# Fused attention and mixture-of-experts block: the exponential tiles' sums without VectorE, with two tiles of a unit added by accumulating DMAs

## Chip, cores and metric

One core of a Trainium2 chip. Time is device microseconds of one execution of the whole program, the median of several runs. Of the engines, PE is the tensor engine, DVE is VectorE, ACT is ScalarE, POOL is GpSimd, and SP is SyncE, which only issues DMAs here.

## What is computed

A transformer block in float32 on x of shape (2, 1024, 512): attention with 16 heads of 32 and low-rank updates on its four projections, a residual and a layer norm; then a mixture of 8 experts (hidden size 704, at most 256 tokens for each) with a shared expert, a residual and a layer norm. The change concerns the softmax of the attention alone:

```python
q = _split(lora_linear(x, Wq, bq, Bq, Aq))
k = _split(lora_linear(x, Wk, bk, Bk, Ak))
v = _split(lora_linear(x, Wv, bv, Bv, Av))
scores = jnp.einsum('bhqd,bhkd->bhqk', q, k) * SCALE
attn = jax.nn.softmax(scores, axis=-1)
out = jnp.einsum('bhqk,bhkd->bhqd', attn, v)
...
x = _layernorm(x + _L0_attn_ref(x, ...), axis=-1)
x = _layernorm(x + _L0_ffn_ref(x, ...), axis=-1)
```

## The kernel before

The program has three stages: the projections of Q, K and V; the attention; and the experts with their routing. The attention is cut into 16 units. A unit `u` is four heads (group `g = u // 2`) and half of a batch's queries (512). Its 1024 keys are cut into 8 chunks of 128, and one chunk is a step; `t` counts the steps of all units, 128 in all, with `u = t // 8` and `k = t % 8`.

In a step, for each of the four heads, the tensor engine multiplies keys by queries into a bank `st` (line 604), ScalarE takes the exponential into an SBUF tile `pt` (line 613), and the next head follows. Two heads share a tile of 128 x 1024, so each step makes two tiles, called pair 0 and pair 1; below, "tile j" means the two tiles of step j of a unit. Softmax needs the maximum of each query's row beforehand. It comes from a second product, `s`, 12 steps ahead (`LEAD`; `s1_step`, lines 176 to 197): one matmul of 512 columns per head and step slot into one of three banks, reduced to its maximum by VectorE (line 191). The maxima reach the exponentials as two extra rows of Q, written by `finish_max`.

One step later, `av_step` (line 628) multiplies the tiles by V into the unit's `av` bank; there are two such banks, so that of unit u is also that of unit u - 2. The tiles are also summed over the steps, element by element (`add_step`, line 617): tile 0 is the accumulator itself, tiles 1 to 6 are added to it, 7 is left out (`DIRECT`). `ON_DVE` puts the adds of (step 1, pair 0) and (step 2, pair 1) on VectorE; the other ten of a unit are GpSimd's. The last two units have their own list, `DVE_END`. The adds are issued just behind `av_step`, except that `EARLY`, (1, 0), is issued one step sooner.

At step 3 (`FIN`) of the next unit `finish` (line 651) sums accumulator and tile 7 over the partitions by matmuls with ones into a bank `sm` (line 657). ScalarE copies `sm`, and SyncE sends one row of each head to DRAM and back as 128 x 16. After step 4 (`REC`) VectorE takes the reciprocal (`invert`, line 678), SyncE writes it to DRAM and reads it back broadcast over the partitions (four DMAs). At step 7 `normalize` (line 691) multiplies the `av` bank by it on VectorE, copies it on ScalarE, and subtracts on VectorE (the result is kept as a high and a low part). From unit `RDIR` on the reciprocal is taken of the whole bank by VectorE (line 667) and DRAM is not used.

The tensor engine's order is written by hand: `between[h]` holds what follows head h's `st` matmul in a step. All engines execute in program order. The `pt` tiles come from a pool of `PTB` = 13 buffers of 4 KB per partition. A buffer is free again when its last reader is done, which for most tiles is GpSimd's add. GpSimd's queue also holds one bias add of 128 x 512 in most units (`add_res`, line 707), and, in units 8 to 10, small operations of the first layer norm. Those units also carry the first batch's output projection (`oproj`, from `t` = 65), which reads the normalised units 0 to 7.

Of the kernel before, what the change touches and what calls it, by code (L numbers as in the profile page):

```python
# [2 lines left out]

# [6 lines left out]
F32 = mybir.dt.float32  # L10
# [3 lines left out]
ALU = mybir.AluOpType  # L14
# [4 lines left out]
P = 128  # L19
B, L, D = 2, 1024, 512  # L20
NU = 16
# [11 lines left out]
LEAD = 12  # L33
LATE, OP_ONE = (0,), 1
NS = NU * 8
WARM, WCOL = 4, 256
OPER = 4
PTB = 13
OHB = 3
LOADS = {  # L40
# [11 lines left out]
MAN4 = MAN2 - MAN3  # L52
DIRECT = (7,)
NO_DIR = (NU - 2,)
FIN = 3
REC = 4
XTB = 5
ON_DVE = ((1, 0), (2, 1))
EARLY = (1, 0)
OPROJ_AT = (65, 67, 69, 71, 73, 75, 77, 79)  # L60
RES_AT = tuple(8 * i + 6 for i in range(8)) + (70, 78, 86, 94, 98, 102, 106, 110)
RES_ADD = 3
# [3 lines left out]
W2_END = {2: (0, 1, 2), 3: (3, 4), 4: (5,)}  # L66
W2_AT = {2: (0, 1), 3: (2, 3), 4: (4,), 5: (5,)}
MPJ, MPP = 0, 2
RDIR = NU - 2
FINE, NRME = 2, 4  # L70
DVE_END = {
    NU - 2: ((1, 0), (2, 1), (4, 1), (5, 1), (6, 0), (6, 1), (7, 0), (7, 1)),
    NU - 1: ((1, 0), (2, 0), (3, 0), (4, 0), (5, 0), (6, 0), (6, 1)),
# [20 lines left out]
def kernel(  # L94
# [3 lines left out]
    pe, act, dve, pool, sp = nc.tensor, nc.scalar, nc.vector, nc.gpsimd, nc.sync  # L98

    def f(ap):  # L100
        return ap.bitcast(F32)
# [41 lines left out]
    def load_k(g):  # L143
        kt = Ks[g % 2]
        for blk, hl in ((0, 0), (1, 1), (2, 0)):
            sp.dma_start(
                out=f(kt[32 * blk : 32 * blk + 32]),
                in_=qk_d[1, g // NG, g % NG, hl].rearrange("(h p) t -> p h t", p=32),
            )
# [13 lines left out]
    def load_q(u):  # L163
        g, qb = u // 2, u % 2
        for blk, hl in ((0, 0), (1, 0), (2, 1)):
            sp.dma_start(
                out=f(Qs[u % 3][32 * blk : 32 * blk + 32]),
                in_=qk_d[0, g // NG, g % NG, hl].rearrange("(h p) t -> p h t", p=32)[
                    :, :, qb * 512 : qb * 512 + 512
                ],  # L170
            )

    mts, pts, avs, accs, vts = {}, {}, {}, {}, {}
# [411 lines left out]
    with ph2, tc.manual_schedule(engines={mybir.EngineType.PE}):  # L585
        ptp = att_left.enter_context(
            tc.tile_pool(name="ptp", bufs=PTB, side="left", reuse_waits="tile")
        )
        ap = ph2.enter_context(
            tc.tile_pool(name="ap", bufs=1, side="right", reuse_waits="tile")  # L590
        )
# [25 lines left out]
        def add_step(t, pr):  # L617
            u, kc = t // 8, t % 8
            if kc == 0:
                accs[u, pr] = pts[t, pr]  # L620
            elif kc not in direct(u):
                eng = dve if (kc, pr) in DVE_END.get(u, ON_DVE) else pool
                eng.tensor_tensor(accs[u, pr], accs[u, pr], pts[t, pr], ALU.add)  # L623

        def early(t, pr):
            return t // 8 not in DVE_END and (t % 8, pr) == EARLY

        def av_step(t):
            u, kc = t // 8, t % 8
            g = u // 2  # L630
            if kc == 0:
                avs[u] = avp.tile([P, 512], F32, name=f"av{u}", tag="av")
            for h in range(4):
                pe.matmul(  # L634
                    avs[u][32 * h : 32 * h + 32, :],
                    vts[g][:, kc, 32 * h : 32 * h + 32],
                    pts[t, h // 2][:, h % 2, :],
                    start=kc == 0,
                    stop=kc == 7,
                    skip_group_check=True,  # L640
                )
            for pr in range(2):
                if not early(t, pr):
                    add_step(t, pr)

        def direct(u):
            return () if u in NO_DIR else DIRECT
# [3 lines left out]
        def finish(u):  # L651
            sm = one.tile([P, 512], F32, name=f"sm{u}", tag="one")
            parts = [lambda h, k_=k_: pts[u * 8 + k_, h // 2][:, h % 2, :] for k_ in direct(u)]
            parts.append(lambda h: accs[u, h // 2][:, h % 2, :])
            for i, pf in enumerate(parts):
                for h in range(4):
                    pe.matmul(
                        sm[32 * h : 32 * h + 32, :],
                        ones32,
                        pf(h),  # L660
                        start=i == 0,
                        stop=i == len(parts) - 1,
                        skip_group_check=True,
                    )
            if u >= RDIR:
                rc = ap.tile([P, 512], F32, name=f"rc{u}", tag="rc", bufs=1)
                dve.reciprocal(rc, sm)
                fin[u] = rc
                return
            rc = ap.tile([P, 512], F32, name=f"rc{u}", tag="rc", bufs=1)  # L670
            act.copy(rc, sm)
            sd = dram.tile([4, 512], F32, name=f"sd{u}")
            sp.dma_start(out=sd, in_=rc[0:P:32, :])
            r16 = ap.tile([P, 16], F32, name=f"r16_{u}", tag="r16", bufs=1)
            sp.dma_start(out=r16, in_=sd.rearrange("h (j c) -> (h j) c", c=16))
            fin[u] = r16

        def invert(u):
            r16 = fin[u]
            rd = dram.tile([4, 512], F32, name=f"rd{u}")  # L680
            dve.reciprocal(r16, r16)
            sp.dma_start(out=rd.rearrange("h (j c) -> (h j) c", c=16), in_=r16)
            rc = ap.tile([P, 512], F32, name=f"rb{u}", tag="rb", bufs=1)
            for h in range(4):
                sp.dma_start(
                    out=rc[32 * h : 32 * h + 32, :],
                    in_=rd[h : h + 1, :].partition_broadcast(32),
                )
            fin[u] = rc

        def normalize(u, parts=(0, 1, 2)):
            g, qb = u // 2, u % 2
            cs = slice(qb * 512, qb * 512 + 512)
            hi, lo = at_h[:, g % NG, cs], at_l[:, g % NG, cs]
            if 0 in parts:
                dve.tensor_tensor(avs[u], avs[u], fin[u], ALU.mult)
            if 1 in parts:
                act.copy(hi, avs[u])
            if 2 in parts:
                dve.tensor_tensor(lo, avs[u], f(hi), ALU.subtract)  # L700

        def load_res(n):
            b, i = divmod(n, 8)
            r0 = b * L + i * P
            sp.dma_start(out=x1[b][:, i, 0:D], in_=x[r0 : r0 + P, :])
# [40 lines left out]
        for t in range(NS):  # L746
            u, k = t // 8, t % 8
            if k == 0:
                if u % 2 == 0 and 2 <= u and u // 2 + 1 < B * NG:
                    load_k(u // 2 + 1)  # L750
                if u >= 1 and u + 2 < NU:
                    load_q(u + 2)
                if u % 2 and NG <= u // 2 + 1 < B * NG:
                    load_v(u // 2 + 1)
            if t in RES_AT:
                load_res(RES_AT.index(t))
            between = [[], [], [], []]
            if early(t, 0):
                between[2].append(lambda: add_step(t, 0))
            if t + LEAD < NS:  # L760
                for q in range(4):
                    between[q].append(lambda q=q: s1_step(t + LEAD, q))
            elif t + LEAD == NS:
                between[0].append(lambda: finish_max(NU - 1))
            if t:
                between[1].append(lambda: av_step(t - 1))
                if u and k == (FINE if u == NU - 1 else FIN):
                    between[1].append(lambda: finish(u - 1))
            if u:
                if k == (NRME if u == NU - 1 else 7):  # L770
                    between[0].append(lambda: normalize(u - 1, (0,)))
                    between[1].append(lambda: normalize(u - 1, (1,)))
                    between[2].append(lambda: normalize(u - 1, (2,)))
            if t - RES_ADD in RES_AT:
                between[3].append(lambda: add_res(RES_AT.index(t - RES_ADD)))
            st_step(t, between)
            if k == REC and 1 <= u < NU - 1:
                invert(u - 1)
            if t in OPROJ_AT:
                op0 = oproj(0, OPROJ_AT.index(t), OPER)  # L780
            if OPROJ_AT[0] <= t:
                next(op0, None)
            if t + 1 in OPROJ_AT[1:]:
                run(op0)
            for _, fn in [x for x in later if x[0] == 0]:
                fn()
            later[:] = [(n - 1, fn) for n, fn in later if n]
            if t - NS >= OPROJ1:
                next(op10, None)
        av_step(NS - 1)  # L790
        finish(NU - 1)
        normalize(NU - 1, (0,))
        run(op10)
# [301 lines left out]
    for st in range(NB):  # L1095
# [18 lines left out]
        if st == NB - 3:  # L1114
            reads_xd(
                sp.dma_start(
                    out=meta, in_=xd_d[:, D : D + 2].rearrange("(j p) c -> p j c", p=P)
# [7 lines left out]
    with tc.manual_schedule(engines=MAN4):  # L1125
        last = None
        for e in range(E):
            nxt = e + 1
            hss = []
            for c in range(6):  # L1130
# [40 lines left out]
                if e:  # L1171
                    for hf in range(2):
                        j = 2 * (e - 1) + hf
# [9 lines left out]
        for hf in range(2):  # L1183
            j = 2 * (E - 1) + hf
# [65 lines left out]
```

## Time and profile before

| | us |
|---|---|
| median of 3 runs | 1081.89 |
| lowest and highest | 1078.75, 1085.99 |
| the profiled execution, and its span | 1070.33, 1068.6 |
| attention, from the first `st` to the last `av` matmul | 157 to 627 |

| engine | busy us of the span | share |
|---|---|---|
| tensor engine (matmuls) | 1038.4 | 97% |
| VectorE | 747.8 | 70% |
| GpSimd | 574.7 | 54% |
| ScalarE | 530.4 | 50% |

These shares are over three stages with different limits. The slices of the page divide the span by 40, so that one digit is 26.7 us, about one unit of attention; a digit is the busy share in tenths. A row of a group gives line, engine, operation, output and inputs with their shapes, the count, then busy time and mean duration in ns, then the engine's idle time just before these instructions and what ended it. The granted clock of the tensor engine is 0.991 of full speed in the mean. Matmuls are pipelined: an `st` or `s` matmul shows 0.40 us, but the next one starts 0.235 us after it.

### The profile page before, as it was taken

The page shows a single profiled execution, that of the slowest core. Times are in us where ns is not written, and L with a number is a line of the kernel's source. Part 1 is how long each engine was busy: PE and PEld are TensorE (multiplying, and loading weights), DVE is VectorE, ACT ScalarE, POOL GpSimd, SP SyncE. Part 2 cuts the span into 40 slices and gives each one's busy share as a digit, 9 for nine tenths or more (in the row PEclk, how much of TensorE's full clock was granted, in tenths as well). Part 3 has the DMA queues.
Part 4 walks back from the last instruction along what each step waited for, and adds up shares of the span by engine and source line. Part 5 has one row for each costly group of instructions (what it writes and reads, how often), then busy time and mean ns, then how long its engine had stood idle before and what let it go on. Part 6 is the DMA issues. An engine that isn't in the chain of part 4 may idle for free. (4 is left out here: it accounts for less than half of the span.)

```text
span 1068.6 us, 16466 instructions
## 1 busy us (share of the span) xinstructions
PE 1038.4 (97%) x5994; PEld 744.8 (70%) x5994; DVE 747.8 (70%) x1217; ACT 530.4 (50%) x1026; POOL 574.7 (54%) x379
## 2 busy tenths in 40 slices
PE   8999999999999999999999999999999999999996
PEld 6888774444444455554444358889999999999995
DVE  6732787899999987889999785333532457777762
ACT  5422214666666655556666656222322356665552
POOL 5000007888888887768998577000050026776674
PEclk9999998999999999999999999999999999999999
DMA  9866860141414242043520113000073356677731
GB/s 301 278 220 202 256 190 21 42 105 47 110 51 110 71 111 71 15 97 71 120 81 22 52 40 127 23 10 21 21 236 120 108 168 228 241 251 258 251 104 60
DMA packets 77585, 131.24 MB, mean 123 GB/s; under 512 B 14344, under 2 KB 23048, under 8 KB 77504
## 3 DMA queue, kind: packets, MB, share of 16 engines
q1 hardware_dynamic: 73664, 117.59, 37.1%
q0 software_dynamic: 3840, 12.60, 3.2%
q8 instruction: 47, 0.77, 0.3%
q14 instruction: 34, 0.28, 0.1%
HBM read 96.10 MB, written 33.80 MB: 122 GB/s over the span
## 5 line engine op out<-in xcount | busy, mean ns | idle before, releaser
L623 POOL TENSOR_TENSOR pt<-pt,pt 128x1024 f32<-128x1024 f32 x151 | 360.4, 2413 | 206.3 <-ACT pt L613 189.1
L191 DVE TENSOR_REDUCE mt<-s 128x1 f32<-128x512 f32 x512 | 323.8, 681 | 42.5 <-PE s L183 42.4
L613 ACT ACTIVATE pt<-st 128x512 f32<-128x512 f32 x512 | 270.9, 602 | 144.1 <-PE st L604 140.3
L604 PE MATMUL st<-qs,ks 98*128 98x512 f32 x512 | 216.4, 433 | 1.9 <-ACT pt L613 1.2
L183 PE MATMUL s<-ks,qs 96*128 96x512 f32 x512 | 204.1, 406 | 12.8 <-DVE mt L191 11.9
L604 PEld LDWEIGHTS st<-qs,ks 98*128 98x128 f32 x512 | 96.5, 190 | 137.3 <-issue 89.1
L864 PE MATMUL h<-xthe,w13s 128*128 128x256 f32 x704 | 129.9, 284 | 0.0
L183 PEld LDWEIGHTS s<-ks,qs 96*128 96x128 f32 x512 | 97.9, 191 | 41.4 <-DVE mt L191 26.9
L852 POOL TENSOR_TENSOR w2s<-w2r,w2s 128x512 fp32r<-128x512 f32 x42 | 65.9, 1592 | 96.9 <-ACT w2s L851 96.7
L864 PEld LDWEIGHTS h<-xthe,w13s 128*128 128x128 f32 x704 | 110.7, 191 | 0.3
L864 PE MATMUL h<-xtle,w13s 128*128 128x256 f32 x352 | 100.2, 285 | 0.0
L623 DVE TENSOR_TENSOR pt<-pt,pt 128x1024 f32<-128x1024 f32 x43 | 91.4, 2132 | 3.4 <-ACT pt L613 2.9
L634 PE MATMUL av<-pt,vt 128*32 128x512 f32 x512 | 75.0, 605 | 0.0
L634 PE MATMUL av<-pt,x1b 128*32 128x512 f32 x512 | 69.9, 619 | 0.0
L1012 POOL DMA_INDIRECT xd_d<-x1a,slot_i x8 | 8.0, 996 | 112.0 <-DVE slot_i L1009 109.9
L864 PEld LDWEIGHTS h<-xtle,w13s 128*128 128x128 f32 x352 | 67.4, 191 | 0.7
L908 PE MATMUL y<-w2s,hs 128*128 128x512 f32 x260 | 60.9, 390 | 0.0
L908 PEld LDWEIGHTS y<-w2s,hs 128*128 128x128 f32 x260 | 48.2, 188 | 10.2 <-DVE hs L890 0.5
L310 PE MATMUL o<-xl,wh 128*128 128x512 f32 x128 | 50.8, 397 | 0.9 <-POOL xl L296 0.9
L310 PE MATMUL o<-xh,wh 128*128 128x512 f32 x128 | 50.7, 396 | 0.8 <-ACT xh L295 0.8
L325 ACT ACTIVATE oh<-o,bqk_sb 128x512 fp32r<-128x512 f32 x32 | 22.0, 690 | 59.1 <-PE o L310 55.9
L310 PE MATMUL o<-xh,wl 128*128 128x512 f32 x128 | 50.5, 394 | 0.0
(822 smaller groups left out, 1760.2 us busy)
## 6 DMA issues: line engine op xcount, KB each, us to landing
qs<-qkd SPq DMA_DIRECT2D x48, 256.0 KB, 5.7
ks<-qkd SPq DMA_DIRECT2D x24, 512.0 KB, 6.9
x1a<-in_w_dram SPq DMA_DIRECT2D x24, 512.0 KB, 6.1
w2r<-in_w_dram SPq DMA_DIRECT2D x42, 256.0 KB, 2.9
qkd<-oh SPq DMA_DIRECT2D x32, 256.0 KB, 2.5
qkd<-ol SPq DMA_DIRECT2D x32, 256.0 KB, 2.5
x1b<-in_w_dram SPq DMA_DIRECT2D x16, 512.0 KB, 4.9
x1b<-in_wT_dram SPq DMA_DIRECT2D x16, 256.0 KB, 5.2
```

The lines of the kernel that those rows point to most:

```text
L183: pe.matmul(s1, Qs[u % 3][0:96, h, qt * P : qt * P + P], Ks[g % 2][0:96, h, kh * 512 : kh * 512 + 512], start=True, stop=True,)
L191: dve.tensor_reduce(mts[u][:, c, kh : kh + 1], s1, AX.X, ALU.max)
L310: pe.matmul(o, lhs, rhs, start=k + i == 0, stop=k + i == KC + 1)
L325: act.activation(oh, o, AF.Identity, bias=bias)
L604: pe.matmul(sb, Ks[g % 2][:, h, kc * P : kc * P + P], Qs[u % 3][:, h, :], start=True, stop=True,)
L613: act.activation(pts[t, h // 2][:, h % 2, :], sb, AF.Exp, scale=SCALE)
L623: eng.tensor_tensor(accs[u, pr], accs[u, pr], pts[t, pr], ALU.add)
L634: pe.matmul(avs[u][32 * h : 32 * h + 32, :], vts[g][:, kc, 32 * h : 32 * h + 32], pts[t, h // 2][:, h % 2, :], start=kc == 0, stop=kc == 7 ...
L852: pool.tensor_tensor(hl[:, 1, :], raw, f(hl[:, 0, :]), ALU.subtract)
L864: pe.matmul(hp[:, j * 256 : j * 256 + 256], lhs, rhs[:, k, :], start=n == 0, stop=n == 11,)
L908: pe.matmul(o, lhs, rhs, start=n == 0, stop=n == 16)
L1012: sc_ = pool.indirect_dma_start(out=xd_d, out_offset=bass.IndirectOffsetOnAxis(ap=slot_i[:, i : i + 1], axis=0), in_=x1[i // 8][:, i % 8, ...
```

## The change

The adds of each unit but the last two follow a table: `ADDS[kc]` lists the tiles whose adds are issued behind `av_step` of step kc. Tile 2 (both pairs) is not added to the accumulator: an accumulating DMA, issued from GpSimd, adds it into tile 3 after step 3's `av` matmuls have read that tile, and tile 3, which then holds both, is added by GpSimd after tile 4. So GpSimd has ten adds and two DMA issues in a unit, VectorE none. In unit 13 three tiles go by DMA (2 into 3, 4 into 5, 6 into 7), with six adds left for GpSimd. `finish` moves from step 3 to step 4, `invert` from after step 4 to after step 5, `normalize` from step 7 to step 0 of the unit after; unit 13 takes its reciprocal directly. `PTB` becomes 14, and the broadcast reciprocal uses the buffer that the copy of `sm` used.

```diff
-PTB = 13
+PTB = 14
-FIN = 3
-REC = 4
+FIN, FINQ = 4, 1
+REC = 5
+NRM = 0
-ON_DVE = ((1, 0), (2, 1))
-EARLY = (1, 0)
+ON_DVE = ()
+ON_DMA = {NU - 3: (2, 4, 6)}
+ADDS = {0: (0,), 1: (1,), 3: (2,), 4: (4,), 5: (3,), 6: (5,), 7: (6,)}
+ADDS_END = {0: (0,), 1: (1,), 3: (2,), 5: (4, 3), 7: (6, 5)}
...
-RDIR = NU - 2
-FINE, NRME = 2, 4
+RDIR = NU - 3
+FINE, NRME = 2, {NU - 2: 7, NU - 1: 4}
...
-            for pr in range(2):
-                if not early(t, pr):
+        def adds(t):
+            u, kc = t // 8, t % 8
+            if u in DVE_END:
+                for pr in range(2):
                     add_step(t, pr)
+                return
+            for j, pr in product((ADDS_END if u in ON_DMA else ADDS).get(kc, ()), range(2)):
+                i = u * 8 + j
+                if j in ON_DMA.get(u, (2,)):
+                    pool.dma_start(out=pts[i + 1, pr], in_=pts[i, pr], accum_op=ALU.add)
+                else:
+                    add_step(i, pr)
...
-            rc = ap.tile([P, 512], F32, name=f"rb{u}", tag="rb", bufs=1)
+            rc = ap.tile([P, 512], F32, name=f"rb{u}", tag="rc", bufs=1)
...
-            if early(t, 0):
-                between[2].append(lambda: add_step(t, 0))
...
                 between[1].append(lambda: av_step(t - 1))
+                between[3 if NS - 16 < t < NS - LEAD else 1].append(lambda: adds(t - 1))
                 if u and k == (FINE if u == NU - 1 else FIN):
-                    between[1].append(lambda: finish(u - 1))
+                    between[1 if u == NU - 1 else FINQ].append(lambda: finish(u - 1))
             if u:
-                if k == (NRME if u == NU - 1 else 7):
-                    between[0].append(lambda: normalize(u - 1, (0,)))
-                    between[1].append(lambda: normalize(u - 1, (1,)))
-                    between[2].append(lambda: normalize(u - 1, (2,)))
+                for v in [u - 2] * (k == NRM and 1 < u < NU - 1) + [u - 1] * (k == NRME.get(u)):
+                    between[0].append(lambda v=v: normalize(v, (0,)))
+                    between[1].append(lambda v=v: normalize(v, (1,)))
+                    between[2].append(lambda v=v: normalize(v, (2,)))
...
-            if k == REC and 1 <= u < NU - 1:
+            if k == REC and 1 <= u <= RDIR:
                 invert(u - 1)
...
         av_step(NS - 1)
+        adds(NS - 1)
         finish(NU - 1)
```

More of the change, by code (lines that the diff above doesn't have):

```diff
@@ L1 @@
 from contextlib import ExitStack
-from itertools import cycle
+from itertools import cycle, product
 import concourse.bass as bass
@@ L623, in add_step @@
                 eng.tensor_tensor(accs[u, pr], accs[u, pr], pts[t, pr], ALU.add)
-        def early(t, pr):
-            return t // 8 not in DVE_END and (t % 8, pr) == EARLY
         def av_step(t):
```

## The prediction

> **What bounds the kernel now.** I read the slices of the page first, then the costliest groups, then the timeline of one attention unit on the engines, and last the windows around the one place where the clock digit drops.
>
> ```profile
> PE   8999999999999999999999999999999999999996
> ...
> DVE  6732787899999987889999785333532457777762
> ...
> PEclk9999998999999999999999999999999999999999
> ```
>
> Attention runs from 157 to 627 us (slices 6 to 23): the tensor engine is at 9 throughout, but so is VectorE, at 9 or 8. A busy 9 on the tensor engine hides short stalls, so its steps have to be timed. I took the start of every fourth `st` matmul (L604), which is the start of a step. In units 1 to 7 the eight steps of a unit last, within 0.1: 3.08, 3.06, 3.48, 4.80, 3.96, 3.33, 3.06, 3.07; 27.84 us in all. An undisturbed step is 3.06. Step 3 also holds the 16 `sm` matmuls (about 1.73) and step 4 one transpose (0.24). So the tensor engine's own work is 8 x 3.06 + 1.73 + 0.24 = **26.45 us** and 1.39 us of each unit is stall, in steps 2, 4 and 5. The timelines of VectorE and of the tensor engine (start, us, engine, line, operation) show where it comes from:
>
> ```profile
> 283.50 1.28 DVE L191 TENSOR_REDUCE mt<-s 128x1 f32<-128x512 f32 x2
> 284.70 3.36 DVE L623 TENSOR_TENSOR pt<-pt,pt 128x1024 f32<-128x1024 f32 x1
> 287.98 1.27 DVE L191 TENSOR_REDUCE mt<-s 128x1 f32<-128x512 f32 x2
> ```
> ```profile
> 287.83 0.39 PE L604 MATMUL st<-qs,ks 98*128 98x512 f32 x1
> 288.71 0.50 PE L183 MATMUL s<-ks,qs 96*128 96x512 f32 x1 [0.49 <-DVE mt L191]
> ```
>
> While VectorE adds an exponential tile for 3.36 us, no maximum is taken; the three `s` banks fill, and the next `s` matmul starts 0.88 us after its `st` instead of 0.235. VectorE's reduces need only 2.48 us of a step, so without adds it keeps up. GpSimd is the other nearly full engine:
>
> ```profile
> L623 POOL TENSOR_TENSOR pt<-pt,pt 128x1024 f32<-128x1024 f32 x151 | 360.4, 2413 | 206.3 <-ACT pt L613 189.1 <-DVE pt L623 15.9
> ...
> L623 DVE TENSOR_TENSOR pt<-pt,pt 128x1024 f32<-128x1024 f32 x43 | 91.4, 2132 | 3.4 <-ACT pt L613 2.9 <-PE av L634 0.2
> ```
> ```profile
> 245.10:272.90 27.80, 27.19 (x146) 13.06 (x145) 25.76 (x40) 17.77 (x36) 24.70 (x12) 1.00 0.19 49
> ```
>
> In unit 3's window (columns: length, then PE, weight loads, VectorE, ScalarE, GpSimd, clock) GpSimd is busy 24.70 of 27.80, VectorE 25.76. The clock digit hides one event in unit 0:
>
> ```profile
> 170.51 0.40 PE L604 MATMUL st<-qs,ks 98*128 98x512 f32 x1
> 173.09 0.79 PE L183 MATMUL s<-ks,qs 96*128 96x512 f32 x1 [2.18 <-DVE mt L191]
> 173.81 1.94 PE L634 MATMUL av<-pt,x1b 128*32 128x512 f32 x8
> ```
> ```profile
> 178.00:180.00 2.00, 2.00 (x8) 0.93 (x11) 1.67 (x3) 1.37 (x3) 1.68 (x1) 0.50 0.06 18
> ```
>
> A VectorE add of 3.32 us at 169.12 starves the tensor engine for 2.18 us, and its clock is then 0.50 from about 173 to 183: steps 4 and 5 of unit 0 take 7.73 and 5.47 instead of 3.30 and 3.06.
>
> **What the skill says.** The Trainium skill, "SBUF — State Buffer", section on the two separate sides: a VectorE operation with two SBUF inputs and a GpSimd operation that reads SBUF take one port pair as an exclusive lock, and the second waits. The trace agrees: VectorE's add lasts 1.21 us at least, 1.90 in the median and 3.37 at most. "DMA: Bandwidth & Descriptors", section on SWDGE and HWDGE: an accumulating DMA can be issued from GpSimd only, whose cores write the descriptors. The trace has no accumulating DMA; it has GpSimd's indirect ones (below). The same page, anatomy of one DMA, prices a transfer at about 2.0 us + bytes / 436 GB/s. "TensorE: Matmul & The Clock Gate", part on the clock gate: idleness halves the clock until activity returns; the 0.50 after the 2.18 us gap agrees.
>
> **The change part by part.** (1) *VectorE's adds.* Two adds in each of units 0 to 13 go, 28 of 43; the 15 of units 14 and 15 stay. Worth the stalls, not the busy time. Above 26.45 units 1 to 7 have 9.8 us (27.83 + 27.91 + 27.84 + 27.83 + 27.86 + 27.81 + 27.86 - 7 x 26.45). Units 8 to 10 carry 96 output-projection matmuls at 0.235: 107.6 - (3 x 26.45 + 22.6) = 5.7. Units 11, 12 and 13 (27.81, 27.82, 28.28): 4.6. Sum **20.1**. (2) *Unit 0.* Steps 2, 4 and 5 are 0.5, 4.4 and 2.4 above: **7.3**, all behind a VectorE add; 2.2 of it is the stall itself and 4.7 the half clock, which I expect to go with it.
>
> (3) *GpSimd.* It keeps 10 adds in a unit (units 0 to 12): 10 x 2.34 (16.44 / 7 in a chain) = 23.4, one bias add of 1.2, and gains two DMA issues. Nearest row:
>
> ```profile
> L1012 POOL DMA_INDIRECT xd_d<-x1a,slot_i x8: 960/962/1232, 778.3 to 787.4; - x8
> ...
> DMA to landing us min/median/max: 3.4/6.6/8.1
> ```
>
> These are 128 rows as well, start to start 1.27 us. The accumulate reads two sources, so I take 1.2, with 0.6 and 2.0 as bounds. GpSimd then needs 23.4 + 1.2 + 2.4 = **27.0 us** of a unit of 26.45. It falls behind 0.55 in each unit. That is affordable: the issue follows the `av` matmuls of tile 3, done 14.2 us after the unit's start (four steps and 2.0); 2.4 and eight adds later, at 35.3, the unit's last add ends. The next unit's step 4 begins at 26.45 + 12.24 = 38.7, where an exponential first wants its buffer (by my count of the 14, one more than before), and the sums, moved from step 3 to 4, read it at about 40: some 4 us of slack. Units 1 to 7 use 3.9 of it; units 8 and 9 (38 and 40 us) give it back. Cost 0; with an issue of 2.0 us GpSimd needs 28.6, and 7 x 2.15 - 4 = 11 us are lost.
>
> (4) *The landing.* Tile 3 already waits for tile 2's DMA when GpSimd reaches its add, and everything behind it in GpSimd's queue waits too, then the sums, then the tensor engine. Between the first issue and that add lie the second issue and two adds of tile 4: 1.2 + 1.2 + 4.7 = 7.1 us. The scatters of L1012 move half as much and land in 3.4 alone and 6 to 8 when sixteen follow each other. Estimate from the page's price, twice the bytes read: 1.2 + 2.0 + 1.05 MB / 436 GB/s = 5.6. Lower bound 4, upper 11. Taken: in time, cost 0. The queue carries little at that point, since K and Q are loaded at step 0 (landing 5.7 to 6.9 us).
>
> (5) *Normalisation* from step 7 to step 0 of the unit after, one step before its `av` bank is written again. Before, its subtract ended 4.1 us after the start of its step; the same in step 0 reaches 1.05 into step 1, where `av` wants the bank at 1.06. Cost 0.1 to 0.5 a unit; I take 0.2. (6) *Reciprocal* one step after the sums, as before, but the steps between lose their stall: from the sums' end to it 5.9 us become about 5.2, the two small DMAs land at about 4.5, now beside 1 MB of accumulation. VectorE would wait in order with the reduces behind it. Cost 0 to 0.8; I take 0.3. (5) and (6): 12 x 0.5 = **6**.
>
> (7) *Units 13 to 15.* Unit 13 has three DMA pairs and six adds (14.0 + 7.2 us, less than now); its reciprocal becomes one of 3.36 us on VectorE in unit 14, where SyncE loses seven small DMAs and ScalarE a copy of 0.59. VectorE has gaps of 1.4 and 0.8 us near there. Cost 0, bounds -1 and 3; the stall in step 3 of unit 14 (5.95 us) stays, as VectorE's adds there do. After attention nothing changes, and the tensor engine is full there until 1000 us, so what attention gains arrives at the end.
>
> **Sum**: 20.1 + 7.3 - 6 = 21 us off the profiled execution's 1070.3 (span 1068.6): 1049. The median of the runs, 1081.9, is 11.6 above that execution for a reason that this profile cannot show; a clock event like that of unit 0 varies. I take a little less than the whole, 19, off the median: **1063**.
>
> **Rivals.** *(A) GpSimd's issue is dear or its landing late by 1 to 2 us*: a need of 28 to 29 a unit, the slack is used up by unit 3, 7 to 14 of the 21 us are lost: 1068 to 1075. For it: GpSimd is at 24.7 of 27.8 already. Against: the adds' own waits on VectorE (15.9 us in all) go. *(B) Slower: the landing of the accumulation.* Every unit's queue on GpSimd stops at tile 3's add. With a need of N per unit the loss is 7(N - 26.45) - 4 in units 1 to 7 and 2(N - 26.45) - 4 in units 11 and 12 against 21 gained, so it turns at N = 29.7: a stall of 2.7, a landing of about 10 us. At 13 us N is 33, the loss 51, the time about 1112. For it: 8.1 us for a quarter of a megabyte in a crowd; against: 2.8 to 3.4 for the same alone. *(C) The waits moved, not removed*: (5) and (6) at their upper ends, 1.3 x 12 = 16, and the clock event stays (4.7): 27 - 21 = 6 gained, 1076. *(D) The change doesn't do what it says*: the new order would leave the adds on VectorE or the tensor engine without slack; against it, the diff takes all 28 off VectorE, and 0.64 us of stall stands right behind one. Gain under 3, 1080.
>
> **Numbers.** Forecast with chance 0.60: 1054 to 1071. A 0.14, C 0.10, D 0.03, B 0.13. About 1% (10.8 us) is what a measurement of this kernel can tell from no change. Faster by more: the forecast and over half of A, 0.68. Within: the rest of A, C, D and the mild end of B, 0.19. Slower: 0.13. The range reaches from 1052 (no cost in 5 and 6, all of unit 0) to 1084, where B begins.
>
> **What would show it.** Right: units of about 26.5 to 27 us, steps 2 and 5 at 3.1, the 4.8 us step now number 4, no `s` matmul waiting on VectorE, VectorE near 21 of 26.7 us, the clock at 1.00 in unit 0, GpSimd above 95% busy. Wrong: gaps before tile 3's add released by the DMA, `sm` or ScalarE's exponentials waiting on GpSimd, `av` at step 1 waiting on the subtract, or a landing above 9 us.

## The result, and the profile after

| | before | after |
|---|---|---|
| median of 18 runs, us | 1079.67 | 1084.98 |
| lowest and highest | 1076.26, 1086.16 | 1080.61, 1089.43 |
| the profiled execution, its span | 1070.33, 1068.6 | 1084.36, 1082.7 |
| last `av` matmul of attention, us from the start | 627.8 | 627.4 |

The ratio is 1.0043 (95% interval 1.0027 to 1.006): the kernel is 0.4% slower, where 1.7% faster was forecast. The page of the kernel after, the slices that answer to those of before:

```profile
PE   9999999999999999999998999999989999999995
...
DVE  6742788778776877777677984323512467777752
...
PEclk9999999999999999999999999999979999999998
```

VectorE falls from 9 and 8 to 8 and 7 during attention, as meant, and the tensor engine's digits don't show that anything was gained. The costliest groups say that the work moved as planned (line, engine, operation, shapes, count | busy us, mean ns | idle before, releaser):

```profile
L626 POOL TENSOR_TENSOR pt<-pt,pt 128x1024 f32<-128x1024 f32 x147 | 366.0, 2904 | 159.3 <-PE av L634 142.6 <-ACT pt L616 12.2 <-DVE pt L626 3.7
...
L654 POOL DMA_DIRECT2D pt<-pt x32 | 29.4, 1092 | 36.7 <-PE av L634 24.4 <-PE st L607 5.1 <-DVE mt L194 4.9
L626 DVE TENSOR_TENSOR pt<-pt,pt 128x1024 f32<-128x1024 f32 x15 | 29.4, 1972 | 0.5
```

Fifteen adds are left on VectorE. GpSimd waits 24.4 us, in ten waits, before its DMA issue, for the `av` matmuls of tile 3: it has time to spare and is not the bound. The windows of a unit's length that begins 1.7 us into unit 3, of a place in unit 14, and of the place in unit 0 where the clock was 0.50 before (length, then busy time and count of the tensor engine, weight loads, VectorE, ScalarE, GpSimd; clock, DMA share, GB/s):

```profile
242.20:269.30 27.10, 27.10 (x149) 12.90 (x145) 21.64 (x38) 17.88 (x35) 26.36 (x14) 1.00 0.46 102
577.00:581.00 4.00, 4.00 (x15) 1.90 (x15) 2.62 (x6) 1.90 (x4) 2.25 (x2) 0.57 0.43 84
178.00:180.00 2.00, 2.00 (x13) 0.76 (x12) 1.70 (x3) 1.04 (x3) 2.00 (x3) 1.00 1.10 217
```

Unit 0's clock event is gone, and VectorE needs 21.64 us of a unit's length. But slow clock stands in a new place. As before I take the start of every fourth `st` matmul as the start of a step, and sum by unit:

| us | before | after |
|---|---|---|
| unit 0 | 32.7 | 25.6 |
| units 1 to 13 | 386.4 | 385.4 |
| units 14 and 15, to the last `st` | 49.6 | 56.1 |

Unit 0 gained its 7.1; units 1 to 13 gained 1.0 of about 14 to 20; units 14 and 15 lost 6.5. The units are now uneven. Outside units 8 to 10, odd ones take 26.9 to 27.5 (unit 1: 28.8), units 2 and 4 take 28.0, unit 6 takes 30.4, unit 12 takes 31.0. Step 4 is about 5.09 in odd units and 6.14, 6.17, 8.50 and 8.73 in units 2, 4, 6 and 12. The tensor engine's timeline in two of these steps, and in step 1 of unit 14 (start, us, engine, line, operation, then idle time before it and what ended it):

```profile
224.82 0.39 PE L607 MATMUL st<-qs,ks 98*128 98x512 f32 x1
226.03 0.47 PE L186 MATMUL s<-ks,qs 96*128 96x512 f32 x1 [0.82 <-DMA qs<-qkd]
...
336.84 0.47 PE L186 MATMUL s<-ks,qs 96*128 96x512 f32 x1 [1.49 <-DMA qs<-qkd]
...
338.82 3.36 PE L669 MATMUL sm<-pt,ones 128*32 128x512 f32 x16
...
575.90 0.50 PE L186 MATMUL s<-ks,qs 96*128 96x512 f32 x1 [3.43 <-DVE mt L194]
```

The first `s` matmul of a new group's heads waits for a load of Q. In unit 6 the sums behind it then take 3.36 us in place of 1.73: half clock again. SyncE's issues say when these loads start:

```profile
212.41 1.26 SPq L149 DMA_DIRECT2D ks<-qkd  x3
213.71 1.73 SPq L169 DMA_DIRECT2D qs<-qkd  x3
...
558.94 0.54 SPq L685 DMA_DIRECT2D sd<-rc  x1
562.81 0.32 SPq L687 DMA_DIRECT2D r<-sd  x1
...
564.76 0.33 SPq L694 DMA_DIRECT2D rd<-r  x1
566.17 3.20 SPq L697 DMA_DIRECT2D rb<-rd  x4
```

Three loads of 512 KB and three of 256 KB are issued at the start of unit 2 (212.4); the wait for the last ends at 226.0, 13.6 us later. The `s` matmuls of the new group start with step 4. Before, step 4 began 14.4 us into the unit (in units 1 to 7 steps 0 to 3 are 3.08 + 3.06 + 3.48 + 4.80), just behind the loads. After, the sums' 1.73 us and the stalls no longer stand ahead of it, and it begins at 12.4, ahead of them. The loads themselves are hardly slower: in units 2, 4, 6 and 12 their last packets end 12.2, 12.7, 12.2 and 13.9 us after the first issue before, and 12.7, 12.8, 13.0 and 14.3 after. So the accumulations hardly delay them.

The last four of these lines, from unit 13, show the second wait: the write of the sums to DRAM (`sd`) is followed 3.87 us later by the read (`r`). Before it was 1.73 us, as here in unit 2:

```profile
231.37 0.55 SPq L673 DMA_DIRECT2D sd<-rc  x1
233.10 0.33 SPq L675 DMA_DIRECT2D r<-sd  x1
```

The issues on GpSimd's queue, and VectorE's timeline, show what stands between and who waits:

```profile
557.10 1.75 POOL L654 DMA_DIRECT2D pt<-pt  x2 [0.33 <-issue]
...
565.30 1.76 POOL L654 DMA_DIRECT2D pt<-pt  x2 [5.12 <-PE st L607]
...
571.63 1.89 POOL L654 DMA_DIRECT2D pt<-pt  x2
```
```profile
207.93 0.25 DVE L693 RECIPROCAL r<-r 128x16 f32<-128x16 f32 x1 [2.88 <-DMA r<-sd]
...
574.56 0.70 DVE L708 TENSOR_TENSOR av<-av,rb 128x512 f32<-128x512 f32 x1 [3.95 <-DMA rb<-rd]
```

The small DMAs are issued just behind pairs of accumulations of 512 KB each. VectorE waits for `r` eleven times, 12.7 us in all: 0.8 to 0.9 in most units, at most 2.9 (in unit 1, where step 6 becomes 5.09). In the order of step 0 of unit 14 it waits for the broadcast `rb`: 3.95 us, with the maxima queued behind, so that the tensor engine stops for 3.43 us and then runs at half clock (the window from 577).

So three candidates: **loads** of K and Q that are late because the sums moved; **small DMAs** beside the accumulations; the **end**, unit 13's three pairs and the direct reciprocal.

### The profile page after: what moved, and what is told of

It reads as the page before. It is cut to its first block, busy times and chain, and to the rows that moved or that the text cites. A ratio compares the mean times of both kernels' runs of the same rounds, so it can differ in the third digit from the quotient of the medians.

```text
span 1082.7 us, 16473 instructions
## 1 busy us (share of the span) xinstructions
PE 1046.8 (97%) x5994; PEld 745.7 (69%) x5994; DVE 693.6 (64%) x1189; ACT 531.1 (49%) x1025; POOL 592.0 (55%) x407
## 5 line engine op out<-in xcount | busy, mean ns | idle before, releaser
L626 POOL TENSOR_TENSOR pt<-pt,pt 128x1024 f32<-128x1024 f32 x147 | 366.0, 2904 | 159.3 <-PE av L634 142.6
L313 PE MATMUL o<-xh,wl 128*128 128x512 f32 x128 | 50.6, 396 | 0.0
L328 ACT ACTIVATE oh<-o,bqk_sb 128x512 fp32r<-128x512 f32 x32 | 21.9, 689 | 57.5 <-PE o L313 54.3
L654 POOL DMA_DIRECT2D pt<-pt x32 | 29.4, 1092 | 36.7 <-PE av L634 24.4
```

The lines of the kernel that those rows point to most:

```text
L313: pe.matmul(o, lhs, rhs, start=k + i == 0, stop=k + i == KC + 1)
L328: act.activation(oh, o, AF.Identity, bias=bias)
L654: pool.dma_start(out=pts[i + 1, pr], in_=pts[i, pr], accum_op=ALU.add)
```

## The experiments

Ratios are to the kernel before on the same chip, with 95% intervals. "Last `av`" is the end of the last `av` matmul in the profiled run; it leaves out what comes after attention (the last section tells why).

| run | ratio | units 1 to 13 | units 14, 15 | last `av` |
|---|---|---|---|---|
| before | 1 | 386.4 | 49.6 | 627.8 |
| after | 1.0043 (1.0027 to 1.006) | 385.4 | 56.1 | 627.4 |
| e1b_noadd | 0.9807 (0.9783 to 0.9831) | 371.9 | 49.4 | 606.9 |
| e2_fin3 | 0.9938 (0.9916 to 0.9961) | 372.3 | 58.0 | 615.0 |
| e3_plain13 | 0.9993 (0.9976 to 1.0011) | 384.5 | 54.3 | 623.6 |
| e_after2 | one run, 1069.91 us | 382.4 | 56.1 | 624.5 |
| e4_k2 | 0.9981 (0.9966 to 0.9996) | 379.9 | 55.6 | 620.8 |
| e5_fin3_plain13 | 0.9906 (0.9884 to 0.9928) | 372.6 | 56.1 | 614.1 |
| e6_late14 | 0.9912 (0.989 to 0.9934) | 372.8 | 57.0 | 614.3 |
| e7_dve13 | 0.9946 (0.9926 to 0.9966) | 381.0 | 52.3 | 620.7 |
| e8_dve13_rt | 0.993 (0.9911 to 0.9949) | 380.9 | 50.6 | 616.0 |
| e9_dve13_own | 0.9944 (0.9923 to 0.9964) | 381.3 | 50.6 | 617.5 |
| e10_gaps12 | 0.9905 (0.9882 to 0.9927) | 373.9 | 54.9 | 614.2 |
| e11_gaps13 | 0.9921 (0.99 to 0.9943) | 372.4 | 55.6 | 612.9 |

### What VectorE's adds cost (e1b_noadd)

The kernel before, without VectorE's 28 adds of units 0 to 13:

```diff
+            elif u not in DVE_END and (kc, pr) in ON_DVE:
+                return
```

ScalarE's copy of the sums also adds 1 to them, so that none is zero.

> The kernel before with VectorE's two adds of units 0 to 13 left out and put nowhere else: those two half tiles are missing from the softmax sums, and 1 is added to each sum by ScalarE's copy so that no sum is zero. Nothing else moves: this is what the adds cost by themselves. Theory, that they are worth what terms 1 and 2 of the prediction say (20 and 7 us) and that the change loses it elsewhere: units 1 to 7 near 26.6 instead of 27.84, unit 0 near 25.6, 20 to 27 us faster than before where the kernel before has its half clock, some 14 to 20 where it has not. Rival, that K and Q land late here too as soon as the steps are shorter: even units keep a stall of 1 us or more in step 4 and the gain is under 12 us.

Ratio 0.9807: the median was 1060.57 against 1079.73 on the same chip. Unit 0 took 25.6, units 1 to 7 took 26.72 to 26.81 each, and the last `av` came 20.9 us sooner. The prediction's starting point holds in kind: the adds on VectorE do cost the tensor engine time. Of the stalls in units 1 to 13, 14.5 us were theirs.

### The sums back at step 3 (e2_fin3)

The kernel after, with two numbers of the kernel before:

```diff
-FIN, FINQ = 4, 1
-REC = 5
+FIN, FINQ = 3, 1
+REC = 4
```

> The changed kernel with the sums back in step 3 and the reciprocal after step 4 (FIN 3, REC 4), all else as changed. Theory, that the move of the sums to step 4 lets step 4 of the even units start 1.7 us before their K and Q have landed: the stalls of 1.0 to 1.9 us and the half clocks in step 4 of units 2, 4, 6 and 12 go, these units fall from 28.0, 28.0, 30.4 and 31.0 to about 26.9, the reciprocal has a step more before normalisation, and the run is 8 to 12 us faster than the change. Rival, that the sums need step 4 because GpSimd is behind: the sm matmuls of step 3 wait on GpSimd's adds by 1 us or more in each unit, and the run is no faster than the change or slower.

Units 1 to 13 fall from 385.4 to 372.3, within 0.4 us of the kernel without the adds, no `s` matmul waits for a load any more, and VectorE waits for `r` once, 0.20 us. The tensor engine's timeline at step 4 of unit 2, and SyncE's and GpSimd's issues in that unit:

```profile
222.99 0.39 PE L607 MATMUL st<-qs,ks 98*128 98x512 f32 x1
223.22 0.40 PE L186 MATMUL s<-ks,qs 96*128 96x512 f32 x1
```
```profile
208.95 1.32 SPq L149 DMA_DIRECT2D ks<-qkd  x3
...
222.70 0.55 SPq L685 DMA_DIRECT2D sd<-rc  x1
224.42 0.33 SPq L687 DMA_DIRECT2D r<-sd  x1
```
```profile
225.61 1.75 POOL L654 DMA_DIRECT2D pt<-pt  x2 [0.46 <-issue]
```

The `s` matmul at 223.22 follows its `st` by 0.23 us; it is 14.3 us behind the issue of the loads. And `sd` and `r` are 1.72 us apart again, both ahead of the accumulations at 225.61. One move of the sums, with the reciprocal behind them, by one step did both harms. What e2 leaves is the end: units 14 and 15 take 58.0 against 49.6, and VectorE still waits 4.33 us there for `rb`.

### Unit 13 with one pair (e3_plain13), and the kernel after again (e_after2)

With `ON_DMA` empty, unit 13 is treated like units 0 to 12: ten adds on GpSimd, one pair of DMAs.

```diff
-ON_DMA = {NU - 3: (2, 4, 6)}
+ON_DMA = {}
```

> The changed kernel with unit 13 adding like all others (one DMA pair and ten adds of GpSimd instead of three pairs and six). Theory, that the broadcast reciprocal of unit 12 lands late because two more pairs of accumulating DMAs of unit 13 stand before it on the DMA engines: VectorE's wait of 3.95 us and the 8.6 us step 1 of unit 14 go (to about 3.3), 4 to 6 us faster than the change, less what GpSimd's four more adds delay unit 14's own adds. Rival, that normalisation in step 0 is late by itself: the wait stays at 3 us or more.

> The changed kernel as it is, for a second profile. Theory for the 12 us lost at 789 to 801 us after attention (the tensor engine idle for no wait shown, then half clock, while the scatters run): it is not caused by the change and comes and goes between executions; here it may or may not be there. Rival: it belongs to the change and is there again at the same place. The step 4 stalls of units 2, 4, 6 and 12 and step 1 of unit 14 are there again in either case.

Step 1 of unit 14 went from 8.64 to 3.28, and the wait for `rb` from 3.95 to 0.15 us: the three pairs were its cause. But steps 3 and 4 then took 6.25 and 7.81, and unit 14 as a whole 31.5 as in the kernel after. VectorE's timeline shows why:

```profile
577.26 4.06 DVE L626 TENSOR_TENSOR pt<-pt,pt 128x1024 f32<-128x1024 f32 x1
581.24 2.47 DVE L194 TENSOR_REDUCE mt<-s 128x1 f32<-128x512 f32 x4
```

An add that takes 1.21 us alone lasted 4.06. GpSimd, whose adds of unit 13 now end 10 us into unit 14 (5 us before), was still at work without a gap. The stall moved from the DMA to the adds. The repetition of the kernel after, on the same chip as e2 and e3, shows the same late step 4 in units 2, 4, 6 and 12 (5.47, 6.00, 6.37, 6.75) and 8.78 in step 1 of unit 14.

### Fewer bytes in the loads (e4_k2)

To part the two harms of the sums' move, the kernel after without the third block of K's rows for the later groups, half a megabyte of some 2.3 (the scores of these groups then lack a part).

```diff
-        for blk, hl in ((0, 0), (1, 1), (2, 0)):
+        for blk, hl in ((0, 0), (1, 1), (2, 0))[: 2 if g > 1 else 3]:
```

> The changed kernel with the third of K's three row blocks not loaded from group 2 on (it keeps what an earlier group left there, so the scores of those units are wrong in their low part): 0.5 MB less of 2.3 MB in the even units. Theory, that the loads' landing is what step 4 of the even units waits for: the loads end some 2 us sooner, the stalls of step 4 in units 2, 4 and 12 (6.0, 6.1, 8.7 us) fall to the 5.1 of the odd units, unit 6 too or nearly, 4 to 7 us faster than the change, level with or slightly faster than before. Rival, that these stalls come from VectorE's wait for the reciprocal: they stay.

Step 4 of units 2, 4, 6 and 12 is 5.09, 5.10, 5.07 and 5.09, as in odd units, and the loads' last packets now end 10.0 to 10.5 us after the first issue in units 2, 4 and 6: the loads' lateness was what made these steps long. In the kernel after they hold 9.2 us more, half clock in units 6 and 12 included; in its repetition, where neither has it, 4.2. Units 1 to 13 as a whole fell only by 385.4 - 379.9 = 5.5 us, because later steps grew: step 6 of unit 6 from 3.09 to 4.46, steps 6 and 7 of unit 12 from 3.52 and 3.32 to 4.76 and 4.81, with a half clock there. What stays above e2 is 379.9 - 372.3 = 7.6 us, most of it in these steps and in step 6 of unit 1 (5.07). So the two harms together are 385.4 - 372.3 = 13.1 us (10.1 in the repetition); how they divide differs by execution. VectorE's waits in this run (total, times, longest):

```profile
DVE r L693 <- DMA r<-sd: 14.8, 11, 2.9
```

### Both repairs, and unit 14 (e5_fin3_plain13, e6_late14)

e5 has the edits of e2 and e3, and takes unit 13's sums one step later, at step 4 of unit 14:

```diff
-                if u and k == (FINE if u == NU - 1 else FIN):
+                if u and k == (FINE if u == NU - 1 else FIN + (u == NU - 2)):
```

> The changed kernel with sums in step 3 (step 4 for unit 13 alone) and reciprocal after step 4, and with unit 13 adding like all others. Theory, that these are two separate faults of the change: units 1 to 13 near 26.8 as with the sums in step 3 alone, step 1 of unit 14 near 3.3 instead of 8.8, and unit 14's other stall in step 4 (3.9 us, the long reciprocal of unit 13 ahead of the last maxima) gone; but GpSimd's adds of unit 13 end some 5 us later in unit 14 than before, so VectorE's own adds of unit 14 wait for the port and 2 to 5 us of stall stay there. 10 to 14 us faster than before, 15 to 19 than the change. Rival, that the stall in unit 14 only moves to another step: no faster than the sums in step 3 alone (7 us).

e6 further issues VectorE's first two adds of unit 14 behind step 3's:

```diff
+                late = {1: (1, 0), 2: (2, 1)} if u == NU - 2 else {}
...
+                    if late.get(kc) != (kc, pr):
...
+                if kc == 3 and u == NU - 2:
+                    add_step(u * 8 + 1, 0)
+                    add_step(u * 8 + 2, 1)
```

> The one before this, with VectorE's adds (1, 0) and (2, 1) of unit 14 issued after step 3's add, when the maxima of the last unit are done or nearly so. Theory, that in unit 14 only adds ahead of the maxima stall the tensor engine: unit 14 falls by 2 to 5 us against the run before, total 12 to 18 us faster than before. Rival, that the adds are then late for what follows, or the buffers they hold stop ScalarE: unit 14 or 15 gets longer by as much.

e5 beats both kernels, at 0.9906. Its unit 14 is 33.2, steps 3 and 4 take 7.91 and 7.24, behind a VectorE add of 5.73 us. In e6 unit 14 falls to 28.9, but step 0 of unit 15 takes 8.18, where `av` waits for an exponential. The sum of units 14 and 15 is 57.0 against 56.1: moving VectorE's adds only moves the stall.

### What VectorE's late adds wait for (e7 to e11)

e7 is e2 with `ON_DMA` empty and VectorE's two adds back in unit 13, so that GpSimd has ten adds there and no DMA, as in the kernel before. e8 is e7 with `RDIR = NU - 2`. e9 is e8 with (2, 0) for (2, 1).

```diff
+    NU - 3: ((1, 0), (2, 1)),
```

> The changed kernel with the sums at step 3 again, no accumulating DMAs in unit 13, and VectorE adding tiles (1,0) and (2,1) of unit 13 as the kernel before did. It asks why units 14 and 15 still take 54 to 56 us in every variant against 47.7 before. Theory P: GpSimd has too much left from unit 13 (14 adds of 2.34 us are 32.8 us in a unit of 26.75), so VectorE's adds of unit 14 come late; with two adds fewer, unit 13 takes about 28.0 (VectorE's adds stall it again), unit 14 27 to 28 and unit 15 20.9, 5 us less than the 81 us that units 13 to 15 took with the sums at step 3 and no DMAs in unit 13: ratio 0.985 to 0.987. Theory R: the direct reciprocal of unit 13's sums, 3.36 us on VectorE in unit 14, is what costs: then steps 3 and 4 of unit 14 still hold 5 us or more above 3.06 and 4.8, and the ratio stays at 0.990 to 0.991.

The count in this text is wrong: GpSimd had ten adds and a pair of DMA issues in unit 13 of the earlier variant, not fourteen adds. It has ten adds here too, so only the two issues went.

> The kernel of the run before this one, with unit 13's reciprocal by way of the small DMAs as in the kernel before (the direct one only from unit 14 on). Theory P: no difference beyond 1 us, ratio 0.984 to 0.987. Theory R: unit 14 goes back to 26.9 us only here, and this run beats the one before it by 3 us or more; units 13 to 15 at 76 us as in the kernel before, ratio 0.984 to 0.986. If units 14 and 15 stay at 54 here too, both are wrong and something that all the variants share, such as the normalisation of unit 12 in step 0 of unit 14, is the cause.

> The kernel of the run before this one with one edit: VectorE's second add of unit 13 is of tile (2,0) instead of (2,1), so that both are in the chain of half 0, and no add of VectorE waits for one of GpSimd's. In the run before, the add of (2,1) lasted 7.79 us in unit 13, because GpSimd, whose queue still held unit 12's last adds, had not yet done (1,1); step 3 of that unit took 13.8 us instead of 4.8. Theory P (an adder that waits in the middle of VectorE's queue stops the maxima, and so the tensor engine): step 3 of unit 13 back to 4.8 to 6, unit 13 at 27 to 28.5, units 14 and 15 at 48 to 50, 7 to 9 us less than the run before: ratio 0.985 to 0.987. Rival: GpSimd's lateness only moves on to the next add that VectorE takes over, in unit 14 or 15, which then holds 5 us or more, and the ratio stays at 0.990 to 0.993.

In e8 units 14 and 15 are back at 50.6, near the 49.6 of before; in e7, with the direct reciprocal, they take 52.3, and step 4 of unit 14 takes 6.58 against 3.38. But the time was only moved: step 3 of unit 13 took 13.41 in e7 and 13.80 in e8, where 4.79 is usual, and the intervals of the two ratios overlap. Neither theory's ratios came. My reading for e9, that VectorE's add waited for a sum that GpSimd had not done, fell: with the add in its own chain the step took 13.75. VectorE, the tensor engine and GpSimd in e9:

```profile
537.16 7.76 DVE L627 TENSOR_TENSOR pt<-pt,pt 128x1024 f32<-128x1024 f32 x1
```
```profile
545.58 0.79 PE L187 MATMUL s<-ks,qs 96*128 96x512 f32 x1 [6.64 <-DVE mt L195]
```
```profile
532.89 7.61 POOL L627 TENSOR_TENSOR pt<-pt,pt 128x1024 f32<-128x1024 f32 x3
539.90 1.64 POOL L722 TENSOR_TENSOR x1b<-x1b,bo_bc 128x512 f32<-128x512 f32 x1
540.95 6.19 POOL L627 TENSOR_TENSOR pt<-pt,pt 128x1024 f32<-128x1024 f32 x2
```

GpSimd's rows overlap: the first three adds end at 540.50, when the bias add (539.90) has begun, and that ends at 541.54, when the next add (540.95) has begun. One at a time, such an add begins every 2.34 us but lasts 2.96 (after one pair of DMA issues; 2.38 in the kernel before). The Trainium skill, "SBUF — State Buffer", section on the two separate sides, says that whoever issues first has the shared port pair for its whole instruction. Here the holder's next instruction began before its last had ended, and VectorE got in only after the first GpSimd add whose successor waited, which ended at 543.83; its own add ended 1.09 us later. e3's and e5's long adds end 1.10 and 1.09 us after such an end, too.

e10 tests it: e9 with GpSimd's adds of unit 12 two by two in one half, so that every second one must wait for the one before. With this order goes a second difference: by `ADDS_END` tiles 4 and 5 of that unit are added one step later, together with tiles 3 and 6. GpSimd's row there has no other gap, so the later issue shouldn't matter, but it was not tested alone. e11 does the same in unit 13 of e5.

```diff
-ON_DMA = {}
+ON_DMA = {NU - 4: (2,)}
...
-            for j, pr in product((ADDS_END if u in ON_DMA else ADDS).get(kc, ()), range(2)):
+            own = u in ON_DMA
+            pairs = product(range(2), ADDS_END.get(kc, ())) if own else product(ADDS.get(kc, ()), range(2))
+            for j, pr in (p[::-1] if own else p for p in pairs):
```

> The kernel of the run before this one with GpSimd's adds of unit 12 in another order: two tiles of half 0, then two of half 1, instead of the halves by turns, so that every second add must wait for GpSimd's own add before it. It asks what VectorE's first add of unit 13 waits for: it took 7.76 us there, began while GpSimd had four operations of unit 12 left, and ended 1.1 us after the first of them that the next did not overlap. Theory L: VectorE is let in only where GpSimd has a gap; since the accumulating DMAs, GpSimd's adds overlap (2.96 us each, one begun every 2.34), so a row of them is one long occupation. With a gap of some 0.08 us after every second add, VectorE's first add in unit 13 takes 1.2 to 5.9 us, step 3 of the unit 4.8 to 11 (13.75 in the run before), and the adds behind such a gap last 2.4 instead of 2.96. Rival B: it is the backlog itself, GpSimd coming first as long as it has work, or the data: then the add takes 7 us or more again, step 3 stays above 13, and the ratio at 0.994.

> The changed kernel with the sums at step 3, one pair of DMAs in unit 13 and its sums at step 4 of unit 14 (the best so far, 0.9906), and GpSimd's adds of unit 13 in the order of two tiles of half 0, then two of half 1. There VectorE's first add of unit 14 took 5.73 us while GpSimd ran unit 13's last adds, and steps 3 and 4 took 7.91 and 7.24. Theory L: with a gap in every second add it takes 1.2 to 4 us, steps 3 and 4 of unit 14 together 2 to 5 us less, and the ratio is 0.986 to 0.989. Rival B: 5 us or more again, steps 3 and 4 at 15 together, ratio 0.990 to 0.992.

VectorE and GpSimd at the same place in e10:

```profile
536.87 2.47 DVE L627 TENSOR_TENSOR pt<-pt,pt 128x1024 f32<-128x1024 f32 x1
539.26 2.47 DVE L195 TENSOR_REDUCE mt<-s 128x1 f32<-128x512 f32 x4
541.65 2.04 DVE L627 TENSOR_TENSOR pt<-pt,pt 128x1024 f32<-128x1024 f32 x1
```
```profile
526.27 15.29 POOL L627 TENSOR_TENSOR pt<-pt,pt 128x1024 f32<-128x1024 f32 x6
```

VectorE's add takes 2.47 us in place of 7.76, step 3 takes 6.39 in place of 13.75, and unit 13 takes 28.4 in place of 35.7. But units 14 and 15 rise from 50.6 to 54.9, so that more than half of the gain is lost again. GpSimd was busy all the while. Its adds, taken singly, lasted 3.03 before the first such gap of 0.08 us and 2.38 after it. Theory L stands. One point of it goes too far: a true gap isn't needed. In e11 VectorE's add, begun at 565.64, ended at 568.75, 1.09 us behind a GpSimd add (to 567.66) that its successor (from 567.62) overlapped by 0.04 us, as its adds do in the kernel before. What shuts VectorE out is the long overlap, 0.6 us in e9 and 1.2 in e5. In e11 VectorE's add fell from 5.73 to 3.10 and step 3 of unit 14 from 7.91 to 5.29. But step 4 stayed at 7.58, step 0 of unit 15 rose from 2.83 to 4.92, and units 14 and 15 gained 0.5 us: mechanism right, the time not. At 0.9921 it can't be told from e5, and neither can e10 at 0.9905. The 6 us that units 14 and 15 still lack in e5 I put down to GpSimd's lateness, whose adds of unit 13 end 12.3 us into unit 14 there (5.3 before); that isn't shown, for no run removed them without a price elsewhere.

## Why the prediction was wrong

Forecast for attention: -21 us (-20.1 - 7.3 + 6). Measured at the last `av`: -0.4.

- **(2) Unit 0**: right in this execution. 7.1 of 7.3; stall and half clock went together. In part that is luck: e7, without these adds too, has a half clock in unit 0, which takes 27.0.
- **(1) VectorE's adds**: right in kind, too large. e1b shows 14.5 in units 1 to 13, not 20.1. I had counted all time above 26.45 as theirs; without the adds units 1 to 7 still take 26.76 and units 8 to 10 still 104.5.
- **(3) and (4), GpSimd's issue and the landing**: right at cost 0 up to unit 12. The two issues of a pair begin 0.57 us apart (estimate 1.2), the packets of a pair end in most units 6.7 us after its first issue and so 6.1 after its second (estimate 5.6), and GpSimd waited for a landing once, 0.4 us. Rivals A and B are out.
- **The step that failed is the move of the sums**, which the forecast put at nothing: (3) counts it only as slack for GpSimd, and (4) sets the loads aside in the sentence "The queue carries little at that point, since K and Q are loaded at step 0 (landing 5.7 to 6.9 us)". Those are medians of single DMAs. The six of a group are one queue of 2.3 MB, whose last wait ends 13.6 us after the unit begins, and their deadline is step 4, which then stood 14.4 us into the unit with the sums ahead of it. The change moved the sums behind that deadline and took away the stalls in front, so step 4 came at 12.4. The wait that took the stalls' place is 9.2 us in step 4 itself, half clock included (4.2 in the repetition), and 5.5 net by e4.
- **(5) and (6)**: 6 us forecast, 7.6 by e4 against e2, in other places than I thought. It is not the normalisation (e2 is within 0.4 us of e1b over units 1 to 13). The waits of 0.8 to 0.9 us for `r` in most units cost the tensor engine little (unit 3 of the kernel after takes 0.35 more than in e2); the cost lies in single units where VectorE waits 1.4 to 2.9 us for `r` behind an accumulation. Rival C named this kind of wait.
- **(7) Units 13 to 15**: cost 0 forecast with 3 as the bound, measured 6.5. I had counted seven small DMAs saved on SyncE and not looked where those of unit 12 would run: behind unit 13's three pairs (step 1 of unit 14, 5.6 us longer). Nor had I asked how late GpSimd would be: without the extra pairs (e3) units 14 and 15 still take 54.3. And "after attention nothing changes" is wrong by 2.6 us: GpSimd's last DRAIN takes 7.91 in place of 5.31 (last section).

Sum of the measured terms: -7.1 - 14.5 + 13.1 (loads and reciprocal together) + 6.5 and +1.3 before attention (158.0 against 156.7, not explained) = -0.7, near the -0.4 seen. Undoing the one move of the sums (e2) makes the change a gain of 0.6%, and with unit 13's extra pairs undone and its sums a step later (e5) of 0.9%. The medians differ by 5.3 us the wrong way, 5.7 more than the last `av` does. Of these, 2.6 are the DRAIN; the other 3 stay open. Beyond their DRAIN, ten of the eleven other runs with a median gain 1.1 to 3.8 us less in it than at the last `av` (e7 gains 0.6 more). So the one profiled execution of the kernel before may have been longer in attention than its usual one, by unit 0's half clock for instance; it has no second profile that could show it.

## What to carry to other kernels

A transfer has a deadline at its first reader, and work that stands ahead of that reader is its cover: before moving such work, or removing stalls ahead of it, take the landing of the last DMA of the batch, not the median of one. Where a small DMA round trip has a reader waiting, issue it ahead of a large accumulation and not behind it. When an adder is taken off one engine, look at how late the other runs at the end of the stage, where the two meet again.

## What the runs showed of the hardware

**GpSimd's instructions overlap after it issues DMAs.** An add's record lasts 2.38 us without them, 2.96 after a pair (unit 12 of e9) and 3.54 in unit 13 of e5, while one begins every 2.34 all the same. A row of them that overlap by 0.6 us or more shuts VectorE's two-input adds out until one waits; e10's gaps of 0.08 us were enough, and so were the 0.03 to 0.04 us of overlap that remain without DMAs. Why they overlap isn't shown; a wait on its own result ended it in e10.

**Each accumulating DMA costs a little at the very end.** Behind the last output DMA GpSimd executes a DRAIN, and the program ends some 0.8 us after it. The instructions of the kernel's last lines, before and after (count, then shortest, median and longest in ns):

```profile
L1246 POOLq DRAIN  x3: 45/102/5312, 1062.5 to 1068.3; - x3
```
```profile
L1258 POOLq DRAIN  x3: 51/102/7908, 1074.0 to 1082.4; - x3
```

The longest takes 5.31 us in the two profiles without accumulating DMAs (before, e1b), 7.42 with 26 of them (e7 to e10), 7.58 with 28 (e3, e5, e6, e11) and 7.91 with 32 (the kernel after, its repetition, e2, e4): 0.081 us for each, though all had landed long before.

**Half clock after shorter stalls.** The Trainium skill, "TensorE: Matmul & The Clock Gate", the two states, gives an idle window of about 3.4 us before the clock halves. Here it followed gaps of 1.49 us (336.84) and of 2.18 in the kernel before. Nor does the length of one gap decide. Before the same matmul of unit 1 the tensor engine waited 1.75 us in the kernel after and 1.71 in its repetition; the clock stayed whole in the first and halved in the second, and steps 6 and 7 took 5.09 and 3.33 against 5.22 and 4.43. The windows of the two:

```profile
210.00:212.00 2.00, 2.00 (x13) 0.83 (x13) 1.72 (x3) 0.81 (x3) 2.00 (x2) 1.00 0.31 95
```
```profile
210.00:212.00 2.00, 2.00 (x11) 0.53 (x10) 1.76 (x3) 1.10 (x2) 2.00 (x2) 0.50 0.29 99
```

So a stall of 1.5 to 2.2 us may bring a half clock behind it or not, and a single profile shows one draw.

**A stop of the tensor engine that has nothing to do with the change.** In some executions of either kernel the tensor engine stops at about 785 to 800 us, where GpSimd scatters tokens and no wait is shown. In the windows of this stretch, the kernel after:

```profile
785.00:800.00 15.00, 10.28 (x47) 6.63 (x45) 1.28 (x3) 0.88 (x3) 10.02 (x11) 0.74 1.00 324
```

and e2 on another chip, 775 to 790, in the same stage:

```profile
775.00:790.00 15.00, 15.00 (x97) 13.65 (x96) 3.52 (x7) 1.61 (x5) 8.06 (x9) 1.00 0.85 282
```

47 matmuls against 97. What follows attention takes 455.2 us in the first, 443.6 in the second. The variants of the kernel after that ran on the chips where the kernel before took 1079 to 1080 all show the long form (453.7 to 455.5; e1b 451.7). Those on the chip where it took 1069 (e2, e3, e_after2) show the short one, 443.1 to 443.7. The profiled execution of the kernel before shows the short one too, 440.8. The kernel after alone has both (455.2 and 443.7), so 11.5 us of the difference between the two profiled executions are no effect of the change, and only ratios on one chip were compared.
